# A two-layer block on one core: outputs added in DRAM, the experts' choice spread out, the states of two units summed together

## The chip, the cores and the metric

The kernel runs on one core of a Trainium2 chip. The core has a matrix engine (PE, with its own queue of weight loads, PEld), a vector engine (DVE), an activation engine (ACT), a general engine (POOL), a queue for transfers (SP), and sixteen DMA engines that all queues share. Each engine takes its own instructions in the order of the program and waits on semaphores for the others. The metric is the time of one execution in microseconds (us) on the device; a shorter time is better.

## What is computed

Four sequences of 256 rows by 512 columns go through two layers. Layer 0 is a latent attention with 32 heads and a gated feed-forward network. Layer 1 is a selective state-space scan and a mixture of low-rank experts, both on the normalized input; their results are added to the input. Cut to layer 1, where the change lies:

```python
xn = layernorm(x)
# scan branch: 1024 channels, 16 states each, 256 steps in order
xc = silu(conv4(xn @ in_proj_x)); z = xn @ in_proj_z
dt, Bm, Cm = ...                      # from xc, normalized
h  = exp(dt * A) * h + dt * Bm * xc   # step after step
ys = sum_n(h * Cm)
y  = ((ys + D * xc) * silu(z)) @ out_proj_w.T
# expert branch: 8 experts of rank 16, the best 2 for each row
base   = xn @ base_W.T
probs  = softmax(xn @ router_W.T); top 2, divided by their sum -> w_dense
inc    = (w_dense * (xn @ lora_A)) @ lora_B
out = x + y + base + 2 * inc
```

## The kernel before

Everything is in float32. The scan of one sequence is cut into 8 chunks of 128 channels, and a chunk into 4 *units* of 4 states; so a sequence is 32 units and the whole scan 128 units. A unit works on a tile of 128 partitions by 4 x 256 elements. Below, "unit s20 of sequence 1" is unit 32 + 20 = 52. The program's order is written out by hand: a table tells, for each sequence `b` and each unit `s`, which functions are issued there. Entries of `put(b, s, f, ...)` are issued at the head of the unit, those of `put_mid` between the unit's two DVE instructions, those of `put_late` after them, and those of `put_end` last. `nxt` is the sequence after `b`, whose projections, convolution and step sizes are made while `b` is scanned.

For each unit the loop at the end of the program issues:

- `decays` (L968, ACT): four exponentials, issued three units ahead into one of four buffers;
- `scan_in` (L983, DVE): first a wait for everything that the scan needs, then the product `bx` (L991) of the B rows (`brow`, in PSUM) and the step inputs (`dus`, brought from DRAM by SP);
- `scan` (L996, DVE): the scan itself, `h <- decay, bx` (L1005), then on POOL the product of the states with the C rows, `h <- h, cr` (L1010);
- `states_sum(u - 1)` (L1016, PE): four matmuls in 32-column tiles (L1022) that add the states of the unit before into `ysum` in PSUM; the first unit of a chunk also starts the sum with a full-width matmul `ysum <- xc, dgs` (L1020). After a chunk's last unit `take_sum` (L1025, ACT) copies `ysum` out, and POOL multiplies it with the gate (L1030).

The states `h` lie in four buffers in turn. So the wait at the head of `scan_in(u)` asks, among other things, that the sum of unit u - 4 be done:

```python
for j in (*first, made["da", u], made["hc", u - 4], made["sum", u - 4]):
    tc.add_manual_dep(i.ins, j.ins.name, early, reason="the scan's waits")
```

Around the scan lie, on the same engines: for `nxt`, `norm_stats` (DVE), `px_mm` (L759, PE, input projections), `conv_in` and `conv_taps` (L806, the convolution as matmuls with diagonals that ACT makes), `conv_silu` (L822, ACT, one Silu over the whole sequence), `pp_mm` (L833, PE, at units s17 and s18, from the Silu's result), `pp_square` and `pp_norm` (L847, DVE, at s21); `step_in`, `step_exp`, `step_out`, `step_x`, `send` and `spread` make the step sizes on ACT and POOL and send them through DRAM on the SP queue.

The experts: `router` (L1036) gives scores and low-rank products for two sequences at a time. `route_exp` (s23) and `route` (s25) choose the experts for two sequences, in b = 0 and b = 2, as one run of DVE instructions between two units; `route` also weighs the low-rank products (`mid`, L1089). One output block is a group of 128 rows; there are eight. Its PSUM tile `po` takes, over many units, `dense` (L1109, four matmuls), `expert_out` (L1112: one matmul with the identity that adds `x`, one with `lora_B`) and `out_mm` (L1117, eight matmuls, one for each chunk), and is then copied by `out_x` to SBUF and stored once. Every such float32 matmul is two passes in the profile. The pool of these PSUM tiles (`psmm`) has three buffers, which all the projections share.

Of the kernel before, what the change touches and what calls it, by code (L numbers as in the profile page):

```python
# [8 lines left out]
F32 = mybir.dt.float32  # L9
# [8 lines left out]
P = 128  # L18
# [23 lines left out]
def block_kernel(  # L42
# [675 lines left out]
    def norm_stats(b):  # L718
        mv = w1.tile([P, 2, 2], F32, tag="mv1", name="mv1", bufs=2)
        for i in range(2):  # L720
            st = w1.tile([P, 6], F32, tag="st1", name="st1", bufs=2)
            nc.vector.bn_stats(st, x[:, 2 * b + i, :])
            nc.vector.bn_aggr(mv[:, i, :], st)
        rs = w1.tile([P, 2], F32, tag="rsn", name="rsn", bufs=2)
        inv_root(rs, mv[:, :, 1], eps[:, 0:1])
        live["ln", b] = mv, rs
# [319 lines left out]
    m1 = w1.tile([P, NR], F32, name="m1")  # L1046
    b2 = w1.tile([P, NR], F32, name="b2")
    ex = w1.tile([P, NR, NE], F32, name="ex")
    sel2 = w1.tile([P, NR, NE], F32, name="sel2")
# [5 lines left out]
    def first_of(out, tmp, val, top):  # L1055

        nc.vector.tensor_reduce(top, val, AX.X, ALU.max)
        nc.vector.tensor_tensor(tmp, val, over(top), ALU.is_equal)
        nc.vector.tensor_tensor(tmp, tmp, rev, ALU.mult)
        nc.vector.tensor_reduce(m1, tmp, AX.X, ALU.max)  # L1060
        nc.vector.tensor_tensor(out, tmp, over(m1), ALU.is_equal)

    def route_exp(b):
        lg = live["ml"][:, :, 0:NE]
        nc.vector.tensor_reduce(m1, lg, AX.X, ALU.max)
        nc.vector.tensor_tensor(ex, lg, over(m1), ALU.subtract)
        nc.scalar.activation(ex, ex, AF.Exp)

    def route(b):

        w = psx.tile([P, NG, S], F32, tag="bx", name="w")
        m2 = w[:, 0, 0:NR]
        sel, best, tmp = (
            w[:, k, 0 : NR * NE].rearrange("p (i e) -> p i e", e=NE) for k in (1, 2, 3)
        )
        first_of(sel, sel, ex, m2)

        nc.vector.scalar_tensor_tensor(best, sel, -4.0, ex, ALU.mult, ALU.add)
        first_of(sel2, tmp, best, b2)
        nc.vector.tensor_tensor(sel, sel, sel2, ALU.add)  # L1080
        nc.vector.tensor_tensor(sel, sel, ex, ALU.mult)
        nc.vector.tensor_tensor(m2, m2, b2, ALU.add)
        nc.vector.reciprocal(b2, m2)

        nc.vector.scalar_tensor_tensor(sel, sel, 2.0, over(b2), ALU.mult, ALU.mult)
        for n in range(2):
            mid = act.tile([P, 2, NE, LR], F32, tag="mid", name="mid", bufs=2)
            for i in (2 * n, 2 * n + 1):
                nc.vector.tensor_tensor(  # L1089
                    mid[:, i % 2], live["ml"][:, i, NE:].rearrange("p (e r) -> p e r", r=LR),  # L1090
                    sel[:, i, :].unsqueeze(2).to_broadcast([P, NE, LR]), ALU.mult,
                )
            live["mid", b + n] = mid
# [17 lines left out]

    def expert_out(b, i):  # L1112
        mm(live["po", b, i], lhsT=ident, rhs=x[:, 2 * b + i, :], start=False, stop=False)
        mm(live["po", b, i], lhsT=live["mt"][:, i * P : (i + 1) * P], rhs=late_w["lb"],
           start=False, stop=False)

    def out_mm(b, i, c):  # L1117
        mm(live["po", b, i], lhsT=xcs[b][:, c, i * P : (i + 1) * P], rhs=late_w["ow"][:, c, :],  # L1118
           start=False, stop=(c == DC - 1))

    def out_x(b, i, side=0):
        tb = 2 * b + i
        (nc.vector.tensor_copy if side else nc.scalar.copy)(x[:, tb, :], live.pop(("po", b, i)))
        (nc.scalar if side else nc.sync).dma_start(out_d[tb * P : (tb + 1) * P, :], x[:, tb, :])
# [413 lines left out]
```

## Time and profile before

| | |
|---|---|
| median of 5 runs | 836.7 us (836.08 to 838.71) |
| the profiled execution's own time | 836.34 us |
| its span, first to last instruction | 834.6 us |
| busy: PE / DVE / ACT / POOL | 748.9 / 654.7 / 554.2 / 496.8 us |
| first `bx` to the last scan's end (the scan phase) | 326.15 to 826.2 us |
| DVE busy from 440 to 466 us | 25.48 of 26 us |
| weight transfer issued from POOL (256 KB) | 0.556 us of POOL each |

The span is what lies between the first and the last instruction; the execution's own time has 1.74 us more around it. The profile names a group by its line, its engine and its tiles (out <- in), then how often it ran, its busy time, the mean of one in ns, and the idle time of its engine just before it with what ended that idle time. Busy time is no proof of a bound: PE is counted busy for 90% of the span, and it waits in order like all others. The timeline view gives start, duration and, in brackets, the idle time just before and its releaser.

### The profile page before, as it was taken

What the parts mean: (1) busy time and instruction counts of PE and PEld (TensorE: products, weight loads), DVE (VectorE), ACT (ScalarE), POOL (GpSimd) and SP (SyncE); (2) the same over time, 40 slices, a digit from 0 to 9 for tenths busy, and PEclk for the clock granted to TensorE, in tenths of its full rate; (3) what the DMA queues carried; (4) which work ended last, traced back from release to release, by engine and by line L of the source; (5) the groups of instructions that cost most, each with busy time, mean ns of one, the idle gap of its engine ahead of it and who ended that gap; (6) DMA issues with size and microseconds to landing.
All of it is one profiled execution on the core that took longest, in us unless ns stands there. A gap on an engine that the chain in (4) does not pass through costs nothing.

```text
span 834.6 us, 11274 instructions
## 1 busy us (share of the span) xinstructions
PE 748.9 (90%) x3846; PEld 429.8 (51%) x3846; DVE 654.7 (78%) x604; ACT 554.2 (66%) x1124; POOL 496.8 (60%) x390
## 2 busy tenths in 40 slices
PE   4999999999999999989897899898999978976885
PEld 2665545666555676656553357444457544422331
DVE  4486755288634535798689999989999889999996
ACT  4335574435556277599896898778898787776560
POOL 3233322001343333677968799859899769798775
PEclk9899999999999999979999999889999998898997
DMA  7233332001222322555394745424654443444410
GB/s 227 64 102 114 89 101 63 1 1 38 77 76 78 117 57 64 150 121 147 95 222 126 177 131 135 127 62 116 164 160 122 110 100 97 107 126 128 113 26 26
DMA packets 68645, 86.72 MB, mean 104 GB/s; under 512 B 12222, under 2 KB 52170, under 8 KB 68459
## 3 DMA queue, kind: packets, MB, share of 16 engines
q1 hardware_dynamic: 58794, 65.81, 30.4%
q0 software_dynamic: 9072, 18.35, 7.9%
q10 hardware_dynamic: 720, 1.84, 0.6%
q8 instruction: 30, 0.49, 0.3%
q14 instruction: 29, 0.23, 0.1%
HBM read 66.58 MB, written 10.22 MB: 92 GB/s over the span
## 4 chain that ended last, share of the span: by engine, by line
PE 50%; DVE 22%; POOL 8%; ACT 7%; DMA 6%; issue 5%; SPq 1%; ACTq 0%; POOLq 0%; DVEq 0%
DVE h L1005 10%; PE pg L444 7%; DVE bx L991 6%; PE pu L444 5%; PE px L759 5%; POOL h L1010 4%; PE av L397 4%; PE ysum L1022 3%; PE po L1118 3%; DMA dus<-dud 3%; PE po L469 3%; PE pz L949 3%; PE px L806 3%; PE scT L386 2%; DVE mpl L354 2%
## 5 line engine op out<-in xcount | busy, mean ns | idle before, releaser
L1010 POOL TENSOR_TENSOR h<-h,cr 128x1024 f32<-128x1024 f32 (+1 forms) x130 | 302.0, 2326 | 71.8 <-DVE h L1005 59.3
L1005 DVE TENSOR_TENSOR_SCAN h<-decay,bx 128x1024 f32<-128x1024 f32 (+1 forms) x129 | 288.1, 2235 | 8.5 <-PE po L469 3.6
L979 ACT ACTIVATE decay<-dts,aneg 128x255 f32<-128x255 f32 x504 | 212.4, 500 | 43.1 <-DVE h L1005 29.4
L991 DVE TENSOR_TENSOR bx<-brow,dus 128x1024 f32<-128x1024 f32 x128 | 157.7, 1232 | 18.8 <-PE ysum L1022 7.7
L1022 PE MATMUL ysum<-h,stack 128*32 128x256 f32 x1024 | 87.4, 416 | 34.6 <-POOL h L1010 34.6
L456 POOL TENSOR_TENSOR hlo<-g,hhi 128x512 fp32r<-128x512 f32 x28 | 35.9, 1281 | 114.2 <-ACT hhi L455 114.2
L354 DVE TENSOR_REDUCE mpl<-sc 128x4 f32<-128x1024 f32 x64 | 76.7, 1219 | 22.4 <-PE sc L352 21.0
L427 POOL DMA_DIRECT2D wgu<-in_wgu x56 | 31.1, 556 | 95.3 <-PE pg L444 94.1
L388 ACT ACTIVATE pe<-scT 128x1024 f32<-128x1024 f32 x64 | 64.0, 1023 | 22.9 <-PE sc L352 14.2
L1118 PE MATMUL po<-ow,xc 128*128 128x512 f32 x128 | 69.9, 653 | 2.0 <-POOL xc L1030 1.6
L1022 PEld LDWEIGHTS ysum<-h,stack 128*32 128x32 f32 x1024 | 21.2, 111 | 93.8 <-POOL h L1010 58.3
L949 PE MATMUL pz<-xn1T,w_in 128*128 128x256 f32 x256 | 69.2, 419 | 0.0
L759 PE MATMUL px<-xn1T,w_in 128*128 128x256 f32 x256 | 61.9, 388 | 0.4 <-ACT sz L955 0.3
L949 PEld LDWEIGHTS pz<-xn1T,w_in 128*128 128x128 f32 x256 | 50.4, 206 | 20.5 <-issue 11.8
L759 PEld LDWEIGHTS px<-xn1T,w_in 128*128 128x128 f32 x256 | 48.2, 192 | 13.8 <-issue 3.9
L452 DVE SCALAR_TENSOR_TENSOR g<-g,pg 128x512 f32<-128x512 f32 x28 | 19.2, 687 | 43.0 <-ACT g L451 43.0
L444 PE MATMUL pg<-xhi,wgu 128*128 128x512 f32 x112 | 49.6, 443 | 1.4 <-ACT xhi L244 1.4
L469 PE MATMUL po<-wd,hhi 128*128 128x512 f32 x112 | 49.3, 440 | 0.0
L444 PE MATMUL pu<-xhi,wgu 128*128 128x512 f32 x112 | 47.3, 423 | 0.8 <-DVE g L454 0.8
L455 ACT CAST hhi<-g 128x512 fp32r<-128x512 f32 x28 | 17.3, 619 | 45.8 <-DVE g L454 45.8
L444 PE MATMUL pg<-xlo,wgu 128*128 128x512 f32 x112 | 45.2, 404 | 0.7 <-DVE xlo L251 0.7
L469 PE MATMUL po<-wd,hlo 128*128 128x512 f32 x112 | 44.3, 395 | 0.0
(237 smaller groups left out, 1277.4 us busy)
## 6 DMA issues: line engine op xcount, KB each, us to landing
dts<-dtd SPq DMA_DIRECT2D x124, 128.0 KB, 3.2
dus<-dud SPq DMA_DIRECT2D x124, 128.0 KB, 3.2
wgu<-in_wgu POOLq DMA_DIRECT2D x56, 256.0 KB, 2.8
w_in<-in_inz SPq DMA_DIRECT2D x16, 512.0 KB, 5.5
w_in<-in_inx SPq DMA_DIRECT2D x14, 512.0 KB, 4.5
dtd<-dt SPq DMA_DIRECT2D x15, 256.0 KB, 2.2
dud<-du SPq DMA_DIRECT2D x15, 256.0 KB, 2.3
wd<-in_wd POOLq DMA_DIRECT2D x7, 512.0 KB, 3.6
```

What stands on the lines that cost most here:

```text
L354: nc.vector.tensor_reduce(mpl2[b % 2][:, qb, 2 * hp : 2 * hp + 2, 16 + 2 * gq : 18 + 2 * gq], sc.rearrange("p i (f k) -> p i f k", f=2), A ...
L388: nc.scalar.activation(pes[b, k][:, 2 * t : 2 * t + 2, :], sc, AF.Exp)
L444: mm(ps, lhsT=wgus[i][:, hc, :], rhs=xs[j][:, hc, :], start=(hc == 0 and j == 0), stop=(hc == HC - 1 and j == 1))
L469: mm(po, lhsT=hids[th][j][:, m, i * P : (i + 1) * P], rhs=wd[:, m, :], start=False, stop=(m == MC - 1 and j == 1))
L759: mm(px[:, i, :], lhsT=w[:, i, hc, :], rhs=xns[b][:, hc, :], start=(hc == 0), stop=(hc == HC - 1))
L949: mm(pz[:, i, :], lhsT=w[:, i, hc, :], rhs=xns[b][:, hc, :], start=(hc == 0), stop=(hc == HC - 1))
L979: made["da", u] = nc.scalar.activation(da[:, k, 1:], live["dts", b, c][:, k, 1:], AF.Exp, scale=aneg[:, c, k, g : g + 1])
L991: nc.vector.tensor_tensor(bx, brow[g // 2][:, g % 2, :].unsqueeze(1).to_broadcast([P, NG, S]), live["dus", b, c], ALU.mult)
L1005: nc.vector.tensor_tensor_scan(h[:, n].rearrange("p n t -> p (n t)"), da[:, n].rearrange("p n t -> p (n t)"), bx[:, n].rearrange("p n t -> ...
L1010: made["hc", u] = (nc.vector if k == NG - 1 else nc.gpsimd).tensor_tensor(h[:, n], h[:, n], crows[b][:, g, :].unsqueeze(1).to_broadcast([P ...
L1022: made["sum", u] = mm(ysum[k * NB : (k + 1) * NB, :], lhsT=stack, rhs=hc[:, k, :], start=False, stop=(g == NU - 1))
L1118: mm(live["po", b, i], lhsT=xcs[b][:, c, i * P : (i + 1) * P], rhs=late_w["ow"][:, c, :], start=False, stop=(c == DC - 1))
```

## The change

1. **Sums in pairs.** After every second unit the sums of the last two units are issued together, instead of one after each unit.
2. **Choice one operation at a time.** `route_exp` and `route` become a generator of fifteen DVE instructions, one issued at a time between or after the two DVE instructions of units s22 to s32. It takes the difference to the best score, and the exponential of one number per row. The low-rank products are weighed on POOL (`expert_mid`), in two instructions for four blocks.
3. **Outputs by accumulating transfers.** For sequences 0 to 2 the block `x` is stored early (`store_x`, SP, in b = 0), and the dense and expert part on the one hand, the output projection on the other, each get a PSUM tile of their own, are copied by ACT and added in DRAM by a transfer from POOL (`add_out`). The identity matmul stays only for the last sequence. `dense`, `expert_turn` and `expert_out` of b - 1 move to units s0 to s3 of b; the `out_mm` of sequences 0 to 2 move to other units.
4. **Smaller moves.** The statistics of sequence 2 (`norm_stats`) move from s0 of b = 1 to s3 of b = 0, and three `step_out` and one `step_x` entry move later.

```diff
     def norm_stats(b):
-        mv = w1.tile([P, 2, 2], F32, tag="mv1", name="mv1", bufs=2)
+        mv = w1.tile([P, 2, 2], F32, tag="mv1", name="mv1", bufs=3)
...
+    def norm_root(b):
...
-    def route_exp(b):
...
-    def route(b):
...
+    def route():
+        vec_ = nc.vector
+        lg = live["ml"][:, :, 0:NE]
+        vec_.tensor_reduce(m1, lg, AX.X, ALU.max)
+        yield
+        vec_.tensor_tensor(dl, lg, over(m1), ALU.subtract)
+        yield
+        vec_.scalar_tensor_tensor(sel1, dl, 0.0, rev, ALU.is_equal, ALU.mult)
+        yield
...
+        vec_.tensor_reduce(b2, dl, AX.X, ALU.max)
+        nc.scalar.activation(e2, b2, AF.Exp)
+        nc.scalar.activation(m1, e2, AF.Identity, bias=1.0)
+        yield
...
+        vec_.scalar_tensor_tensor(sel1, sel1, 2.0, over(m1), ALU.mult, ALU.mult)
+        yield
+
+    def expert_mid(b, n):
+        mid = act.tile([P, 2, NE, LR], F32, tag="mid", name="mid", bufs=2)
+        i = slice(2 * n, 2 * n + 2)
+        nc.gpsimd.tensor_tensor(
+            mid, live["ml"][:, i, NE:].rearrange("p i (e r) -> p i e r", r=LR),
+            sel1[:, i, :].unsqueeze(3).to_broadcast([P, 2, NE, LR]), ALU.mult,
         )
...
+    def store_x(tb):
+        stored[tb] = nc.sync.dma_start(rows_of(tb), x[:, tb, :])
+
+    def add_out(tb, po):
+        nc.scalar.copy(x[:, tb, :], po)
+        d = nc.gpsimd.dma_start(rows_of(tb), x[:, tb, :], accum_op=ALU.add)
+        tc.add_manual_dep(d.ins, stored[tb].ins.name, early, reason="sums in place")
+        stored[tb] = d
+
     def expert_out(b, i):
-        mm(live["po", b, i], lhsT=ident, rhs=x[:, 2 * b + i, :], start=False, stop=False)
-        mm(live["po", b, i], lhsT=live["mt"][:, i * P : (i + 1) * P], rhs=late_w["lb"],
-           start=False, stop=False)
+        po, last = live["po", b, i], b == B - 1
+        if last:
+            mm(po, lhsT=ident, rhs=x[:, 2 * b + i, :], start=False, stop=False)
+        mm(po, lhsT=live["mt"][:, i * P : (i + 1) * P], rhs=late_w["lb"], start=False, stop=not last)
+        if not last:
+            add_out(2 * b + i, live.pop(("po", b, i)))
 
     def out_mm(b, i, c):
+        if c == 0 and b < B - 1:
+            live["po", b, i] = psmm.tile([P, D], F32, tag="mm", name="po2")
...
+        if c == DC - 1 and b < B - 1:
+            add_out(2 * b + i, live.pop(("po", b, i)))
...
-            for c in range(DC):
-                put(b, c // 2, out_mm, b - 1, 1, c)
-            put(b, 3, out_x, b - 1, 1)
-            put(b, 4, dense, b - 1, 0, 0)
-            put(b, 5, dense, b - 1, 0, 1)
-            put(b, 5, expert_out, b - 1, 0)
-            for c in range(DC):
-                put(b, 6 + c if c < 2 or nxt == B else 14 + c, out_mm, b - 1, 0, c)
-            put(b, 15 if nxt == B else 23, out_x, b - 1, 0)
+            put(b, 0, gate_silu, b, 0, 1)
+            for k, u in enumerate((0, 1, 1, 2)):
+                put(b, u, dense, b - 1, k // 2, k % 2)
+            put(b, 2, expert_turn, b - 1)
+            for i in range(2):
+                put(b, 3, expert_out, b - 1, i)
+            for (bo_, i), us in {
+                1: {(0, 0): range(22, 30)},
+                2: {(0, 1): (4, 4, 4, 5, 5, 5, 6, 7)},
+                3: {(1, 0): (4, 4, 4, 5, 5, 5, 6, 6), (1, 1): (6, 7, 7, 7, 8, 8, 8, 9),
+                    (2, 0): (9, 9, 10, 10, 10, 11, 11, 11), (2, 1): (12, 12, 12, 13, 13, 13, 14, 15)},
+            }[b].items():
+                for c, u in enumerate(us):
+                    put(b, u, out_mm, bo_, i, c)
...
+            for tb in range(NTB - 2):
+                put(b, 8 + tb // 2, store_x, tb)
...
-            put(b, 0 if b else 2, norm_stats, nxt)
+            if nxt == 2:
+                put_mid(0, 3, norm_stats, nxt)
+            else:
+                put(b, 0 if b else 2, norm_stats, nxt)
+            put(b, 0 if b else 2, norm_root, nxt)
...
-                put(b, 25, route, b)
-            put(b, 26, expert_turn, b)
-            put(b, 25, dense, b, 1, 0)
-            put(b, 26, dense, b, 1, 1)
-            put(b, 28, expert_out, b, 1)
+                choice = route()
+                for w, u in ((0, 22), (0, 23), (0, 24), (1, 25), (0, 25), (0, 26), (1, 27), (0, 27),
+                             (0, 28), (1, 29), (0, 29), (1, 30), (0, 30), (0, 31), (0, 32)):
+                    (put_mid if w else put_late)(b, u, next, choice)
+                for i in range(2):
+                    put_late(b, 32 + i, expert_mid, b, i)
...
-        if 1 <= u <= total:
+        if u and u % 2 == 0:
+            states_sum(u - 2)
             states_sum(u - 1)
```

## The prediction

> **What bounds the kernel now.** I read the page's groups first, then the waits by engine, then the timeline of DVE and of PE in the scan phase. The groups name the loop's four costs (line, engine, out <- in, count, busy, mean ns, idle before):
>
> ```profile
> L1010 POOL TENSOR_TENSOR h<-h,cr 128x1024 f32<-128x1024 f32 (+1 forms) x130 | 302.0, 2326 | 71.8 <-DVE h L1005 59.3
> L1005 DVE TENSOR_TENSOR_SCAN h<-decay,bx 128x1024 f32<-128x1024 f32 (+1 forms) x129 | 288.1, 2235 | 8.5 <-PE po L469 3.6
> L991 DVE TENSOR_TENSOR bx<-brow,dus 128x1024 f32<-128x1024 f32 x128 | 157.7, 1232 | 18.8 <-PE ysum L1022 7.7
> L1022 PE MATMUL ysum<-h,stack 128*32 128x256 f32 x1024 | 87.4, 416 | 34.6 <-POOL h L1010 34.6
> ```
>
> Undisturbed units follow each other at 3.59 us (`bx` at 523.72, 527.31, 530.89): 1.23 + 2.29 + 0.07. POOL idles mostly until DVE's scan. So DVE bounds the scan phase, and only what lengthens a unit counts. From the first `bx` (326.15) to the last (822.50) lie 127 units, 496.4 us; 127 x 3.588 is 455.7. The excess of 40.7, summed from the starts of `bx`: units 0 to 5 of sequence 0, 8.0; units 6 to 21 of sequence 0, 10.7; the choice at s22 and s24, 4.8 in sequence 0 and 6.3 in sequence 2; s20 and s21, 3.84 in sequence 1 and 2.52 in sequence 2; the statistics at s31, 1.71 and 2.50; the rest 0.3. The waits (total us, times, longest) say who ends them:
>
> ```profile
> DVE bx L991 <- PE ysum L1022: 7.7, 6, 2.3
> DVE bx L991 <- DMA dus<-dud: 5.2, 3, 3.5
> DVE h L1005 <- PE po L469: 3.6, 1, 3.6
> DVE w L1057 <- ACT ex L1067: 1.6, 1, 1.6
> ```
>
> PE is the engine that DVE waits for, though not for want of time alone: in-order PE waits 14.5 us in 8 places for ACT to copy `ysum` out.
>
> **Choice.** The run that goes, in DVE's timeline of sequence 0:
>
> ```profile
> 434.86 0.19 DVE L1057 TENSOR_REDUCE w<-ex 128x4 f32<-128x32 f32 x1
> ...
> 438.27 0.20 DVE L1085 SCALAR_TENSOR_TENSOR w<-w,b 128x32 f32<-128x32 f32 x1
> 438.51 0.88 DVE L1089 TENSOR_TENSOR mid<-ml,w 128x128 f32<-128x128 f32 x4
> 439.42 1.23 DVE L991 TENSOR_TENSOR bx<-brow,dus 128x1024 f32<-128x1024 f32 x1
> ```
>
> Both runs together cost 4.8 + 6.3 = 11.1, the second with 1.57 of waiting for ACT's exponential. Fifteen instructions of 0.20 come back per choice. One lone 0.13 instruction at s1 (`sh`) lengthens its unit to 3.66, by 0.07; the two of s22 (0.16 and 0.19) lengthen theirs by 0.19. So a 0.20 one costs 0.10 to its full 0.20; I take 0.14, nearer the rows: 30 x 0.14 = 4.2 (3.0 to 6.0). **-6.9** (-8.1 to -5.1). The exponential of `b2` on ACT is asked for by the reciprocal three units later; ACT stands three units ahead by its decays, which hides it. `mid` becomes four POOL instructions of the gate's form (L1030, 128x256, 0.727): 2.9 us of POOL, hidden, since POOL has 3.59 - 2.37 = 1.2 free in each unit before side work; without that cover, 2.9.
>
> **Statistics of sequence 2.** 0.66 + 0.18, twice, gave 1.71. At s3 of sequence 0 they delay `scan(3)`, but `scan(4)` waits 3.6 for PE's last `po` (L469), so they cost nothing there; without that wait, 1.7. **-1.7**. The first sums of the loop, issued together, let PE end that `po` some 0.5 sooner: **-0.5** (0 to -1).
>
> **Pairs, the gain.** PE in sequence 1:
>
> ```profile
> 508.78 1.89 PE L806 MATMUL px<-pad,tap 128*128 128x256 f32 x8
> 510.51 1.89 PE L759 MATMUL px<-xn1T,w_in 128*128 128x256 f32 x8
> 512.33 0.64 PE L1022 MATMUL ysum<-h,stack 128*32 128x256 f32 x8
> 512.90 1.99 PE L759 MATMUL px<-xn1T,w_in 128*128 128x256 f32 x8
> ```
>
> Group after group starts 1.73 later; with a sum between, 1.82 + 0.57 = 2.39, so a sum costs 0.66. Of its 0.64 some 0.41 is the idle time to the next full-width load, so a second sum in the same group should add about 0.23: 0.9 for a pair instead of 1.32, 27 us of PE over 64 pairs. It pays only where PE holds DVE up:
>
> ```profile
> 530.11 1.12 PE L1118 MATMUL po<-ow,xc 128*128 128x512 f32 x2
> 534.31 1.22 PE L1020 MATMUL ysum<-xc,dgs 128*128 128x256 f32 x2 [3.07 <-ACT xc L1027]
> ...
> 536.47 3.68 PE L833 MATMUL pp<-xc,xpw 128*64 128x256 f32 x8
> 541.26 1.94 PE L833 MATMUL pp<-xc,xpw 128*64 128x256 f32 x8
> 543.13 0.64 PE L1022 MATMUL ysum<-h,stack 128*32 128x256 f32 x8
> 543.97 1.23 DVE L991 TENSOR_TENSOR bx<-brow,dus 128x1024 f32<-128x1024 f32 x1 [2.35 <-PE ysum L1022]
> 546.39 0.48 DVE L847 SCALAR_TENSOR_TENSOR nrm<-pp,lnw,rs 64x256 f32<-64x256 f32 x1 [1.19 <-ACT rs L715]
> ```
>
> PE stands idle for the copy (3.07), although the Silu that `pp` needs ended at 532.09; then `bx` of s21 waits for the sum of s17, and `nrm` for what follows `pp`. Afterwards L1020 of s16 stands behind both `pp`, and the two `out_mm` of s18 and s19 are gone. `pp` from 532.1: 3.68 + 1.94 = 537.7; L1020 and the sum of s16, about 0.9: 538.6. `bx` of s20 stood at 538.07, so it waits 0.6, s21 and `nrm` no more; `nrm` itself keeps 0.4. 3.84 becomes 1.0: **-2.8** (-3.4 to 0). In sequence 2, where the wait was 2.52: **-1.3** (-2.1 to 0).
>
> **Pairs, the cost.** For even u the sum of u - 4 now comes behind PE's work of one unit more; this speaks against the change. In sequence 0, `bx` of s12 started at 377.59 without a wait, while that of s13 waited for the sum of s9 until 382.88. That sum stands behind the convolution matmuls of s10, which start when ACT has made the diagonals (376.66). Now the sum of s8 stands there too, so s12 starts at about 383.2 and s13 at 386.8, 3.9 later. PE and ACT pace this stage as before; a wait for `dus` (s20, 414.89) swallows some, but the sum of s16 now lies behind both `pp` (413.65, 5.35, cold after 3.9 idle) and L1020, so s20 starts near 420.3 and s21 near 424, not 419.77. **+4.0** (0 if the saved PE time arrives first, +6). In sequences 1 and 2, s11 and s12 hold 1.8 + 3.6 + 1.8 of matmuls and a pair of 0.9: 8.1 in two units of 7.18. **+1.4** each (0 to 4).
>
> **Outputs.** PE loses six identity matmuls of two passes (0.59 each): 7 us, off the path. ACT gets six more copies of 0.576 and the moved `mt` copy. SP's seven stores stay seven, six of them at s8 to s10, ahead of spreads that have units to spare. POOL gets twelve transfers, of which the only row is a plain load:
>
> ```profile
> L427 POOL DMA_DIRECT2D wgu<-in_wgu x56: 527/558/746, 8.5 to 276.1; - x56
> ```
>
> I take 0.56 each, 6.7 in all; no row accumulates, so the cost may lie between 0.56 and the 2.8 that such a load takes to land. At s3 two of them stand behind ACT's copies, and behind them waits POOL's product of s3. The decays of s6 ended in sequence 1 at 1.0 into s4; two copies more make 2.2, so the product ends about 5.7 after its scan, not 2.55. A product had 8.3 to spare before the scan four units on: no cost there.
>
> The Trainium skill ("DMA: Bandwidth & Descriptors", Specifications) gives a first byte after about 1 us for POOL's software path and 0.6 for SP's, which speaks against moving stores to POOL. This case's trace has 0.556 of POOL for the issue. By the page's figure the twelve would hold POOL for 12 us, by the row for 6.7; the sum would be the same by both, as the slack covers either.
>
> ACT: the decays of s7 had 3.34, 1.50 and 1.74 to spare in sequences 1 to 3. Two copies (0.9) and the lost cover of the long choice eat that in two sequences: **+1.5** (0 to 4). In sequence 3, s4 to s13 hold three `out_mm` each: 0.955 x 3 (two take 1.91 at 469.90) + 0.45 + 0.14 = 3.5 of 3.59, where PE was busy 12.4 of 21 us (733 to 754). It just fits: **+0.7** (0 to 4).
>
> **Sum.** -6.9 - 1.7 - 0.5 - 2.8 - 1.3 + 4.0 + 2.8 + 1.5 + 0.7 = -4.2. The profiled execution took 836.34 (its span 834.6 and 1.74 around it), the median of the runs is 836.7; on the median: **832.5**.
>
> **Rivals.**
> - *The freed PE time carries through.* For it: DVE's largest releaser is PE; 27 us and up to 14.5 us of waiting go. Then ACT's diagonals come sooner, and the +4.0, +2.8, +1.5 and +0.7 fall away: -13.2, 823.5. Against it: in sequence 0, ACT was busy without a gap from 353.5 to 372, and PE cannot hurry that.
> - *The even scans decide (slower).* Place: `scan_in` at even units from s8 to s20. It decides once PE ends a pair over 7.18 after the even unit's start. Seq 0 then loses 6, sequences 1 and 2 lose 4 each, and the gain at s20 is nil: -6.9 - 1.7 - 0.5 + 14 + 1.5 + 0.7 = +7.1, 843.8. For it: the sum of s10 had 3.6 to spare at s14, about one unit's work. Against it: PE saves 0.4 in every pair.
> - *POOL is held by the transfers.* If an accumulating issue costs 2 to 2.8, four between s6 and s15 of sequence 3 and the pairs at s3 push products past their 8.3, about +4 on the forecast: 836.7. Against it: the 0.56 row.
>
> **How the numbers follow.** Forecast 0.50, freed PE 0.22, even scans 0.16, POOL 0.12. The forecast's own range, its open terms together, is 827 to 838. The whole range leaves out half of each outer case, about 0.2: 823 to 842. Within 0.2% (835.0 to 838.4) the kernel can't be told from the one before. Faster: 0.40 + 0.22 = 0.62. Same: 0.08 of the forecast and 0.07 of POOL = 0.15. Slower: 0.02 + 0.16 + 0.05 = 0.23.
>
> **What would show it.** Right: no run of small DVE instructions and lone 0.20 ones in units of about 3.7; no statistics at s31 of sequence 0; PE's wait for `ysum`'s copy gone before `pp`; `bx` of s12 and s20 in sequence 0 waiting for sums, at even units. Wrong: waits of `bx` for POOL's product, issues of `out <- x` far over 0.6, or DVE units of 3.59 through all of s8 to s21.

## The result and the profile after

The changed kernel takes 838.5 us (median of 50 runs) beside 836.4 for the kernel before; the ratio is 1.0034, with a 95% interval of 1.0023 to 1.0044. The ratio goes by all runs, and 0.0034 of 836.4 is 2.8 us (the medians alone are 2.1 apart): the change is slower by 2.8 us, where the prediction said faster by 4.2. The profiled execution's span is 837.1 us (834.6 before).

The costliest groups of the loop in the changed kernel's page (busy us, mean ns, idle before):

```profile
L1014 POOL TENSOR_TENSOR h<-h,cr 128x1024 f32<-128x1024 f32 (+1 forms) x130 | 312.1, 2426 | 59.3 <-DVE h L1009 47.3
L1009 DVE TENSOR_TENSOR_SCAN h<-decay,bx 128x1024 f32<-128x1024 f32 (+1 forms) x129 | 288.1, 2235 | 6.2 <-PE po L469 1.6
L995 DVE TENSOR_TENSOR bx<-brow,dus 128x1024 f32<-128x1024 f32 x128 | 157.6, 1231 | 33.1 <-PE ysum L1026 10.8
L1026 PE MATMUL ysum<-h,stack 128*32 128x256 f32 x1024 | 80.3, 413 | 35.6 <-POOL h L1014 35.6
```

PE's sums cost less (80.3 us, 87.4 before), and DVE's scan is untouched. But DVE's idle time before `bx` has gone from 18.8 to 33.1 us. The view of waits (us, times, longest) names several releasers for it:

```profile
DVE bx L995 <- PE ysum L1026: 10.8, 4, 6.6
DVE bx L995 <- ACT dg L780: 6.2, 2, 4.6
DVE bx L995 <- ACT decay L983: 5.1, 4, 3.0
DVE bx L995 <- DMA rl<-in_rl: 2.7, 1, 2.7
```

Of these only the first is right. The diagonals (`dg`), the decays and the load had long been done; in the timeline, from s7 of sequence 0 on, `bx` starts 0.20 to 0.26 us after PE's sum of the unit four back wherever it waits for 0.3 us or more, and every such place is an even unit. The starts of `bx` give the excess over 3.588 us per unit:

| units | before | after |
|---|---|---|
| 0 to 5 of sequence 0 | 8.0 | 7.7 |
| 6 to 21 of sequence 0 | 10.7 | 18.5 |
| s22 of sequence 0 to s0 of sequence 1 (choice, statistics) | 6.5 | 1.9 |
| s1 to s19 of sequence 1 | 0.1 | 3.5 |
| s20, s21 of sequence 1 | 3.9 | 0.3 |
| s22 to s31 of sequence 1 | 2.5 | 3.9 |
| s0 to s19 of sequence 2 | 0.1 | 2.6 |
| s20, s21 of sequence 2 | 2.5 | 0.3 |
| s22 of sequence 2 to s0 of sequence 3 (choice) | 6.4 | 1.0 |
| the rest of sequence 3 | 0.1 | 2.9 |
| all 127 | 40.7 | 42.5 |

What the change was to take out of the choice, the statistics and s20 is gone: 15.8 us. It came back in the convolution stage of sequence 0 (+7.8) and in small waits over sequences 1 to 3.

### The profile page after: what moved, and what is told of

Same layout as the page of the kernel before. It is cut to its first block, busy times and chain, and to the rows that moved or that the text cites. A ratio compares the mean times of both kernels' runs of the same rounds, so it can differ in the third digit from the quotient of the medians.

```text
span 837.1 us, 11252 instructions
## 1 busy us (share of the span) xinstructions
PE 737.7 (88%) x3834; PEld 441.1 (53%) x3834; DVE 649.7 (78%) x590; ACT 557.3 (67%) x1132; POOL 509.6 (61%) x406
## 4 chain that ended last, share of the span: by engine, by line
PE 48%; DVE 18%; ACT 12%; POOL 12%; issue 6%; DMA 3%; SPq 1%; POOLq 0%; ACTq 0%; DVEq 0%
DVE h L1009 7%; POOL h L1014 7%; PE pg L444 6%; PE pu L444 5%; DVE bx L995 5%; PE av L397 4%; ACT decay L983 4%; PE po L469 3%; PE pz L953 3%; PE ysum L1026 3%; PE px L763 3%; PE px L810 2%; PE scT L386 2%; PE po L1119 2%; DVE mpl L354 2%
## 5 line engine op out<-in xcount | busy, mean ns | idle before, releaser
L1014 POOL TENSOR_TENSOR h<-h,cr 128x1024 f32<-128x1024 f32 (+1 forms) x130 | 312.1, 2426 | 59.3 <-DVE h L1009 47.3
L995 DVE TENSOR_TENSOR bx<-brow,dus 128x1024 f32<-128x1024 f32 x128 | 157.6, 1231 | 33.1 <-PE ysum L1026 10.8
L1026 PE MATMUL ysum<-h,stack 128*32 128x256 f32 x1024 | 80.3, 413 | 35.6 <-POOL h L1014 35.6
L1026 PEld LDWEIGHTS ysum<-h,stack 128*32 128x32 f32 x1024 | 25.0, 112 | 82.1 <-POOL h L1014 52.9
L1148 PE MATMUL po<-ow,xc 128*128 128x512 f32 x128 | 64.7, 643 | 0.4 <-DVE xc L1446 0.4
L763 PEld LDWEIGHTS px<-xn1T,w_in 128*128 128x128 f32 x256 | 50.1, 198 | 16.8 <-ACT xn1T L755 6.2
L444 PE MATMUL pu<-xlo,wgu 128*128 128x512 f32 x112 | 44.4, 396 | 0.0
```

The costliest lines, as they stand in the source:

```text
L444: mm(ps, lhsT=wgus[i][:, hc, :], rhs=xs[j][:, hc, :], start=(hc == 0 and j == 0), stop=(hc == HC - 1 and j == 1))
L763: mm(px[:, i, :], lhsT=w[:, i, hc, :], rhs=xns[b][:, hc, :], start=(hc == 0), stop=(hc == HC - 1))
L995: nc.vector.tensor_tensor(bx, brow[g // 2][:, g % 2, :].unsqueeze(1).to_broadcast([P, NG, S]), live["dus", b, c], ALU.mult)
L1014: made["hc", u] = (nc.vector if k == NG - 1 else nc.gpsimd).tensor_tensor(h[:, n], h[:, n], crows[b][:, g, :].unsqueeze(1).to_broadcast([P ...
L1026: made["sum", u] = mm(ysum[k * NB : (k + 1) * NB, :], lhsT=stack, rhs=hc[:, k, :], start=False, stop=(g == NU - 1))
```

## The experiments

Each ratio is to the kernel before, on the same chip, with its 95% interval; 0.001 is 0.84 us. "Excess" is the measure of the table above, from one profile of each run.

**Pairs and transfers, each with and without.** `a_single` puts the sums of single units back, `a_noadd` leaves the accumulating transfers out, `a_single_noadd` does both.

```
-        if u and u % 2 == 0:
-            states_sum(u - 2)
+        if 1 <= u <= total:
             states_sum(u - 1)
```
```
         nc.scalar.copy(x[:, tb, :], po)
-        d = nc.gpsimd.dma_start(rows_of(tb), x[:, tb, :], accum_op=ALU.add)
-        tc.add_manual_dep(d.ins, stored[tb].ins.name, early, reason="sums in place")
-        stored[tb] = d
```

> The changed kernel with one sum after every unit again, all else as changed. Theory 'pairs' (an even unit's sum comes one unit of PE work later, and DVE waits for it): the waits at even units of sequence 0 (18.4 us there after the change, 10.7 before) go back by 7.7, those at s8 and s24 of sequence 1 (2.9 and 2.2), s14 and s20 of sequence 2 (1.7 and 0.9) and s4 to s20 of sequence 3 (2.9) go, some 3 us come back at s20 and s21 of sequence 1: about 828, ratio to before 0.990. Rival 'POOL' (its longer queue makes the products, and so the sums, late): the waits stay whoever issues the sums, 836 to 839, ratio 1.000 to 1.003. Rival 'freed PE' (pairs save PE time and that is worth more than it costs): 841 or more, ratio over 1.005.

> The changed kernel without POOL's accumulating transfers (the outputs lack the sums that they add; the copies to x stay). Theory 'pairs': POOL's issues lie in its slack, no change, 838 within 1, ratio 1.002 to 1.004. Rival 'POOL': the lag of its products (6 to 9 us after the scans at s3 to s12 of sequences 1 and 3, 5 to 6 elsewhere) falls and with it the waits in sequences 1 and 3, -4 to -8, ratio 0.993 to 0.998.

> The changed kernel with single sums and without POOL's accumulating transfers (the outputs lack the sums that they add). If the transfers are the whole cost of the outputs: 825.7, ratio 0.987. If they are half of it, and PE's and ACT's moved work the other half: 829.5, ratio 0.992. If only the moved work costs: 833, ratio 0.996 as with the transfers.

| ratio | pairs | single sums |
|---|---|---|
| with the transfers | 1.0034 (1.0023 to 1.0044) | 0.9959 (0.9941 to 0.9978) |
| without them | 0.998 (0.9958 to 1.0002) | 0.9903 (0.989 to 0.9917) |

Pairs cost 6.3 us with the transfers and 6.4 without; the transfers cost 4.5 with pairs and 4.7 without. Within the intervals, some 2 us for each difference, the two costs simply add. Theory "pairs" had the sign, but with 828 too large a gain; that POOL's issues lie in its slack was wrong.

**Where the pairs cost.** `b_pairs` is the kernel before with pairs alone (the first diff above, reversed). `a_pairs_not0` is the changed kernel with pairs only where `u // PER > 0`:

```
+    summed = 0
...
-        if u and u % 2 == 0:
-            states_sum(u - 2)
-            states_sum(u - 1)
+        if 1 <= u <= total and not (u % 2 and u // PER > 0):
+            while summed < u:
+                states_sum(summed)
+                summed += 1
```

> The kernel before with the sums in pairs alone. Theory 'pairs': +7.7 in sequence 0, less up to 3.6 at s20 and s21 of sequence 1, and some waits at even units elsewhere: 840 to 844, ratio 1.005 to 1.009. The prediction's own terms (-0.5 -2.8 -1.3 +4.0 +2.8) give +2.2, ratio 1.003. Rival 'freed PE': -4.6, ratio 0.994. Rival 'POOL': without the new transfers and copies pairs cost nothing, ratio 1.000 or below.

> The changed kernel with single sums in sequence 0 and pairs in sequences 1 to 3. Theory 'pairs cost in sequence 0 alone': its 7.8 us go, the rest stays as it is in the changed kernel (s8 and s24 of sequence 1, sequence 3, and the gain at s20 and s21): ratio 0.994, below the 0.996 of single sums throughout. Rival 'pairs cost everywhere': half of 6.3 us goes, ratio 0.9995, above single sums throughout.

Measured: 1.0033 (1.0013 to 1.0053) and 0.9942 (0.9923 to 0.9962). Single sums in sequence 0 alone give 7.7 us back, which is what the table shows there, and pairs in the other three sequences gain 1.4 against `a_single`, less than the intervals can tell from nothing. In `b_pairs` the profile has +7.8 in units 6 to 21 of sequence 0, and -3.6, -2.3 at s20 and s21 of sequences 1 and 2; in sequence 2 most of that comes back close by, 2.0 at s19 and 1.8 at s23. Alone, pairs cost 2.8 us, not the 6.3 that they cost in the changed kernel.

How 7.8 us come about is to be read from the first of these waits. PE and DVE in the changed kernel, s7 and s8 of sequence 0 (start, us, engine, line):

```profile
361.84 2.07 PE L876 MATMUL pdt<-nrm,dtw 32*128 32x256 f32 x4 [1.77 <-ACT dt L882]
...
363.84 1.22 PE L1024 MATMUL ysum<-xc,dgs 128*128 128x256 f32 x2
...
364.99 1.94 PE L1026 MATMUL ysum<-h,stack 128*32 128x256 f32 x16
...
366.33 1.23 DVE L995 TENSOR_TENSOR bx<-brow,dus 128x1024 f32<-128x1024 f32 x1 [2.74 <-DMA rl<-in_rl]
```

and the same place in the kernel before:

```profile
360.32 1.08 PE L1022 MATMUL ysum<-h,stack 128*32 128x256 f32 x8
...
361.34 2.07 PE L872 MATMUL pdt<-nrm,dtw 32*128 32x256 f32 x4
...
363.09 1.23 DVE L991 TENSOR_TENSOR bx<-brow,dus 128x1024 f32<-128x1024 f32 x1
...
363.34 1.08 PE L1022 MATMUL ysum<-h,stack 128*32 128x256 f32 x8
```

Before, the sum of s4 ran ahead of `pdt`, and `bx` of s8 (363.09) didn't wait. Now the pair, the sums of s4 and s5, stands behind `pdt`, and `pdt` waits 1.77 us for ACT; the products for the first half of the pair were ready before that. `bx` of s8 waits 2.74 (the load that the view names was not what it waited for: the first half of the pair, the sum of s4, ended 0.26 before it). From there on the stage goes round in waits. PE's waits for ACT and ACT's for PE in the stage, after (356 to 425 us):

```profile
PE pp L837 <- ACT xc L826: 4.9, 1, 4.9
...
PE px L810 <- ACT xc L788: 2.0, 1, 2.0
PE pdt L876 <- ACT dt L882: 1.8, 1, 1.8
...
ACT ml L1047 <- PE pr L1045: 3.2, 1, 3.2
ACT xc L1031 <- PE ysum L1026: 2.9, 2, 2.1
```

and before (356 to 420 us):

```profile
PE pp L833 <- ACT xc L822: 3.9, 1, 3.9
...
PE px L806 <- ACT xc L784: 0.7, 1, 0.7
...
ACT ml L1043 <- PE pr L1041: 2.3, 1, 2.3
ACT xc L1027 <- PE ysum L1022: 1.4, 2, 1.1
```

The view by windows (PE, PEld, DVE, ACT and POOL busy, then the share of its full clock that PE was granted), after and before:

```profile
356.00:425.00 69.00, 57.27 (x309) 40.90 (x310) 49.70 (x30) 59.71 (x132) 52.13 (x33) 0.85 0.57 154
```
```profile
356.00:420.00 64.00, 57.42 (x310) 38.68 (x310) 52.72 (x31) 58.99 (x132) 53.13 (x34) 0.89 0.49 124
```

PE is busy for as long as before to within 0.2 us, ACT to within 0.8; each waits longer for the other. But PE's equal busy time is not equal work. The sums take 8.4 us instead of 9.8, and what they save is lost on the matmuls that follow a wait: `pp` takes 6.0 instead of 5.4, those with the diagonals 8.5 instead of 8.0. In these windows the clock was granted at half rate for 20.5 us after and 13.7 before, and each such stretch that begins in the stage began when PE had been idle for 2.0 to 3.0 of the 3.4 us ahead of it. So longer waits went with a slower PE; by an estimate (half of the 6.8 us more) that is some 3 us of PE's work. The clock's share of the 7.8 us is not separated from that of the waits by any run. Over whole runs, the granted clock was 0.937 on average in the changed kernel and in `b_pairs`, 0.951 in the kernel before and 0.946 in `a_pairs_not0`; in the kernel before too, runs with a lower clock were longer (831.2 us at 0.964, 838.5 at 0.950).

**The choice.** `a_oldchoice` is the changed kernel with the old `route_exp` at s23 and `route` at s25; in it the exponential came behind the step's own at s23. `a_oldchoice2` has it ahead of them, as before. `b_choice_stats` is the kernel before with the new choice and the moved statistics; parts of its edit:

```
+            if b % 2:
+                put(b, 2, expert_turn, b - 1)
...
+                    put(b, 3, expert_out, b - 1, 1)
...
-                put(b, 25, route, b)
+                choice = route()
...
+                    put_late(b, 32 + i, expert_mid, b, i)
```

> The changed kernel with the old choice (a run of DVE instructions at s25, products for mid on DVE), all else as changed. If the choice gains what its own units show (11.1 of excess before, 2.1 after): +9, 847.5, ratio to before 1.013. If it gains the 6.9 predicted: 845.4, ratio 1.011. If the run of the choice only gave slack that is lost elsewhere (PE catches up behind it): +4 or less, ratio under 1.008.

> As a_oldchoice, but the exponential asked for ahead of the step's own, as in the kernel before. If the choice in the changed kernel gains what the old one cost less what the new one costs in its own units (11.1 less 2.1): +9, ratio 1.014. If 2.3 of that was the exponential's place: +6.7, ratio 1.011. If the old run of DVE instructions also gave PE and POOL time to catch up, which the lone instructions don't: +4 or less, ratio below 1.008.

> The kernel before with the new choice (its three neighbours that give it room too: two step_out, one step_x, and the even sequences' turn and second lora product behind the choice) and the moved statistics; sums one at a time and outputs as before. Theory 'outputs' (what the choice and the statistics gain is given back by the outputs' part of the change): -9.0 for the choice, -1.7 for the statistics, 825.7, ratio to before 0.987. Rival 'choice smaller' (the units of the choice hide a cost that appears elsewhere): 0.996, the ratio of the changed kernel with single sums.

Measured: 1.0132 (1.0097 to 1.0167), 1.0103 (1.0083 to 1.0124), and 0.9934 (0.9915 to 0.9952). Within the changed kernel the choice gains 5.8 us; choice and statistics in the old surroundings 5.5. Its own units show more: 11.1 before, 2.1 after. Most lone instructions cost nothing at all, since a unit with one of 0.17 us stays at 3.58; the 2.1 lie in a few that ran far longer. One of them, DVE and POOL in the changed kernel at s27 of sequence 0:

```profile
454.22 1.26 POOL L931 TENSOR_TENSOR du<-dt,xc 128x512 f32<-128x512 f32 x1
454.57 0.96 DVE L1078 TENSOR_TENSOR sel<-dl,b 128x32 f32<-128x32 f32 x1
455.44 2.34 POOL L1014 TENSOR_TENSOR h<-h,cr 128x1024 f32<-128x1024 f32 x1
455.46 1.22 DVE L995 TENSOR_TENSOR bx<-brow,dus 128x1024 f32<-128x1024 f32 x1
```

It ends when POOL's instruction does (455.48, plus 0.05). In `b_choice_stats`, where POOL lags 7.2 us behind the scans at s24 to s26 of sequence 2, the same instruction took 1.91 and the next 0.85, each to 0.05 after the end of a POOL product, and the units of the choice there have an excess of 4.4. What the choice gains is thus not one number: against `outputs_alone2` (below), which has the outputs' part and the old choice, `a_single` with the new choice and the moved statistics gains 11.9 us (1.0101 to 0.9959).

**The outputs alone.** `outputs_alone` and `outputs_alone2` are the kernel before with the outputs' part of the change alone; the second has the exponential in its old place. The second against the first:

```
             put(b, 22, c_rows, nxt, 0)
+            if b % 2 == 0:
+                put(b, 23, route_exp, b)
             put(b, 23, step_exp, nxt, 0, slice(0, 2))
...
-                put(b, 23, route_exp, b)
                 put(b, 25, route, b)
```

> The kernel before with the outputs' part alone (dense products at s0 to s2 of the next sequence, sums stored apart, accumulating transfers on POOL); choice, statistics and single sums as before. Theory 'outputs': +7, 843, ratio 1.008, with POOL's products lagging 6 to 10 us behind their scans from s3 to s17 of sequences 1 to 3. Rival 'no cost there' (the prediction's own step, 0 and +1.5 and +0.7 for ACT and PE): at most +2.2, ratio 1.003 or below.

> As outputs_alone, but the old choice's exponential is asked for ahead of the step's exponentials at s23, as in the kernel before (in outputs_alone it stood behind them, which cost 3.5 and 2.0 us at s24 of sequences 0 and 2). The outputs' part alone: 1.0216 less 5.5 us is a ratio of 1.015. Rival (the prediction's terms for it, +2.2): 1.003.

Measured: 1.0216 (1.0198 to 1.0235) and 1.0101 (1.0076 to 1.0125). The first is spoilt by the exponential. The second says 8.4 us, not the 2.2 of the prediction, and not 12.5 either. Beside the new choice the same part costs only 2.1 (`b_choice_stats` 0.9934 to `a_single` 0.9959). POOL's products end 6.8 to 10.8 us after their scans from s3 to s14 of sequences 1 to 3 (before: 2.5 to 5.2).

**What a transfer on POOL costs.** `b_pooladd` makes seven plain stores of the kernel before accumulating ones on POOL's queue, `b_poolstore` plain ones there. The edit of the second (the first also gives `accum_op=ALU.add`):

```
-        (nc.scalar if side else nc.sync).dma_start(out_d[tb * P : (tb + 1) * P, :], x[:, tb, :])
+        (nc.scalar if side else nc.gpsimd).dma_start(out_d[tb * P : (tb + 1) * P, :], x[:, tb, :])
```

> The kernel before with its seven stores of SP's queue made accumulating transfers on POOL's (the output then holds sums with what lay there before); nothing else is moved. Theory 'a transfer slows POOL': the two to seven products after each issue take 2.6 to 3.0 us instead of 2.35, some 20 of 130 above 2.45, and the time rises little, ratio 1.000 to 1.004. Rival (products are slow in the changed kernel because of what was moved beside them): all products stay at 2.35, ratio 0.998 to 1.001.

> The kernel before with its seven stores of SP's queue on POOL's, plain, without accumulation. Theory 'any transfer on POOL's queue slows POOL': products of 2.6 to 2.7 us for 20 to 30 us after each issue, some 30 of 130 above 2.45, and a ratio near the 1.008 of b_pooladd, half of it at the end, where the last store lands later. Rival 'the accumulation does it': products stay at 2.35 and the ratio is 1.000 to 1.003.

Measured: 1.0079 (1.0051 to 1.0107) and 1.0061 (1.0039 to 1.0083). About half lies at the end: from the last `bx` to the end of the span 15.7 and 15.0 us instead of 12.1, as the last store lands later from POOL's queue. The other half (3.3 and 2.8 us) is in the loop, where POOL stood 12.9 and 16.5 us behind ACT's copies. POOL around its first store, accumulating:

```profile
481.47 0.93 POOL L1127 DMA_DIRECT2D out<-x  x1 [2.21 <-PE ysum L1022]
482.12 5.01 POOL L1010 TENSOR_TENSOR h<-h,cr 128x1024 f32<-128x1024 f32 x2
...
488.00 2.66 POOL L1010 TENSOR_TENSOR h<-h,cr 128x1024 f32<-128x1024 f32 x1
490.32 1.57 POOL L918 TENSOR_TENSOR e<-e,lw 128x512 f32<-128x512 f32 x1
```

and plain:

```profile
480.36 0.61 POOL L1124 DMA_DIRECT2D out<-x  x1 [2.19 <-ACT x L1123]
...
486.88 2.36 POOL L1010 TENSOR_TENSOR h<-h,cr 128x1024 f32<-128x1024 f32 x1
489.20 1.26 POOL L918 TENSOR_TENSOR e<-e,lw 128x512 f32<-128x512 f32 x1
```

The product takes 2.66 by its record in the first and 2.36 in the second, so it is the accumulation, not the queue, that lengthens it. But the next instruction starts 2.32 after it in both. "Slow products", as the expectations have it, is wrong: POOL's pace is unchanged, and only the ends come late.

**How the transfers cost 4.6 us.** `a_single_late` issues each transfer three units after ACT's copy; `a_single_plain` makes the twelve plain.

```
-        d = nc.gpsimd.dma_start(rows_of(tb), x[:, tb, :], accum_op=ALU.add)
...
+        owed.append([3, tb])
...
+            d = nc.gpsimd.dma_start(rows_of(tb), x[:, tb, :], accum_op=ALU.add)
```
```
-        d = nc.gpsimd.dma_start(rows_of(tb), x[:, tb, :], accum_op=ALU.add)
+        d = nc.gpsimd.dma_start(rows_of(tb), x[:, tb, :])
```

> As a_single (0.9959), but each accumulating transfer is issued three units after ACT's copy of its sum, so that POOL doesn't stand behind the copy. Theory 'wait' (POOL in its order behind the copy makes the lag): the lag at s3 falls from 8 to 3 us and the cost of the transfers (0.9959 against 0.9903 without them) goes, 0.991. Theory 'slow products': they stay at 2.6 to 3.0 us for 20 to 30 us, and the ratio stays within 0.994 to 0.996.

> As a_single, but the twelve transfers on POOL's queue are plain stores (the later store of a block overwrites the earlier, so the outputs lack what would be added). As b_poolstore showed, products then stay at 2.35 us and an issue takes 0.58. Theory 'slow products': 0.991 to 0.992. Theory 'wait': 0.994 to 0.996.

Measured: 0.9936 (0.9912 to 0.996) and 0.9944 (0.9926 to 0.9963), between the 0.9959 of `a_single` and the 0.9903 without transfers. Without the wait POOL's lag at s3 falls from 8.3 to 2.5 us as expected, but only some 1.9 us come back. Plain stores, which keep the wait and end the products on time, give 1.3 back, which lies in the range of theory "wait" (0.994 to 0.996) and not in that of "slow products". The late issue brings a loss of its own. POOL and DVE in `a_single_late`, s1 of sequence 2:

```profile
588.94 0.88 POOL L1142 DMA_DIRECT2D out<-x  x1
589.55 1.58 POOL L931 TENSOR_TENSOR du<-dt,xc 128x512 f32<-128x512 f32 x1
...
590.00 3.47 DVE L735 SCALAR_TENSOR_TENSOR sh<-mv,rsn 128x2 f32<-128x2 f32 x1
...
590.78 2.65 POOL L1014 TENSOR_TENSOR h<-h,cr 128x1024 f32<-128x1024 f32 x1
...
593.40 1.22 DVE L995 TENSOR_TENSOR bx<-brow,dus 128x1024 f32<-128x1024 f32 x1
```

The small `sh` (0.13 us in the kernel before) ends only after two of POOL's instructions, and its unit loses 3.3 us, where `a_single` loses 0.3. The excess of the whole loop is 36.6 us; less this place it is 33.3, beside 33.9 without transfers and 36.9 in `a_single`. So by the profiles the wait behind ACT's copies can account for the whole cost. It is worked out from one profile of each, and no run has the late issue without that loss: argued, not shown. PE's view agrees in direction: its sums wait 30.4 us in all for POOL's products in `a_single`, 20.2 without transfers, 25.1 with the late issue (35.6 and 23.4 in the changed kernel with and without transfers).

**Better versions.** `b_best` is `b_choice_stats` with pairs from s16 to s21 of sequences 1 and 2. `a_ident` is `a_single` with identity matmuls and one store on SP in place of the transfers; `a_ident_hyb` adds pairs from s8 to s21 of sequences 1 and 2, `a_ident_hyb2` of sequence 2 alone.

```
         if c == 0 and b < B - 1:
             live["po", b, i] = psmm.tile([P, D], F32, tag="mm", name="po2")
+            mm(live["po", b, i], lhsT=ident, rhs=x[:, 2 * b + i, :], start=True, stop=False)
...
         if c == DC - 1 and b < B - 1:
-            add_out(2 * b + i, live.pop(("po", b, i)))
+            out_x(b, i)
```

> The kernel before with the new choice, the moved statistics, and pairs only from s16 to s21 of sequences 1 and 2; elsewhere one sum after every unit, outputs as before. Theory 'pairs cost where PE paces the conv stage of sequence 0 and pay where pp stands behind the copy': the 3.6 and 2.3 at s20 and s21 come on top of 10.7: 820, ratio 0.980. Rival (the pairs' gain there needs the outputs' products gone from s18 and s19): 824 to 826, ratio 0.985 to 0.987.

> The changed kernel with single sums, and with identity matmuls in place of the accumulating transfers: expert_out adds x as before and is copied to x by ACT, the first out_mm of a block adds that x again, and one store on SP's queue sends the sum; places of the dense products and of out_mm as in the changed kernel. If the transfers cost what the two pairs of runs show (4.6 us) and 12 identity matmuls of 0.6 lie off the path: ratio 0.990 to 0.992. Rival (PE is near its bound there): the 7 us of PE count in part, 0.995 or more.

> As a_ident, with the sums in pairs from s8 to s21 of sequences 1 and 2 alone. If pairs gain where pp stands behind the copy and PE had saved time before it (the kernel before with pairs: 3.6 and 2.3 us at s20 and s21): 0.984 to 0.987. Rival (pairs move the wait from s20 and s21 to s19, as in b_best, or to s13): the ratio of a_ident.

> As a_ident, with the sums in pairs from s8 to s21 of sequence 2 alone. In a_ident_hyb's profile the pairs lost 2.0 at s19 and 3.4 at s23 of sequence 1 and saved 2.7 in sequence 2. Theory 'pairs pay where no out_mm lies near pp': 0.986 to 0.987. Rival (a_ident_hyb gained by its pairs in sequence 1 too): 0.988 or more.

Measured: 0.9925 (0.9905 to 0.9945), 0.9895 (0.9871 to 0.9919), 0.9871 (0.9845 to 0.9896) and 0.9863 (0.9837 to 0.9888). `b_best` gains nothing over `b_choice_stats` that its interval shows: the waits go from s20 and s21 to s19 (2.5 and 4.6 us in sequences 1 and 2). With the output products moved away and the transfers gone, `a_ident` beats the kernel before by 1.0% and the changed one by 1.4%, and `a_ident_hyb2`, 825.3 us beside 836.0, by 1.4%. What is left to wait for in its profile:

```profile
DVE bx L995 <- PE ysum L1026: 7.8, 8, 2.4
DVE bx L995 <- DMA dus<-dud: 5.4, 4, 3.5
DVE bx L995 <- ACT decay L983: 1.7, 1, 1.7
```

## Why the prediction was wrong

The runs form a ladder from the kernel before to the changed one: `b_choice_stats` 0.9934, `a_single_noadd` 0.9903, `a_single` 0.9959, the change 1.0034. Each rung beside the prediction's terms for it (us):

| part | predicted | measured |
|---|---|---|
| choice and statistics (-6.9 -1.7) | -8.6 | -5.5 |
| outputs without the transfers (ACT +1.5, sequence 3 +0.7) | +2.2 | -2.6 |
| transfers | 0 | +4.7 |
| pairs (-0.5 -2.8 -1.3 +4.0 +2.8) | +2.2 | +6.3 |
| sum (of unrounded terms) | -4.2 | +2.8 |

Each measured rung is uncertain by some 2 us, and the ladder is one order of several. Alone on the kernel before, pairs cost 2.8 (`b_pairs`), close to the predicted 2.2, and the outputs with their transfers 8.4 (`outputs_alone2`) where the ladder has 2.1; choice and statistics gain 5.5 there and 11.9 on top of the outputs. The prediction added the parts as if each had one price, and they don't. That the pairs' 2.2 was met when alone is luck: its parts were +7.8 for +4.0 in sequence 0, -5.9 for -4.1 at s20 and s21, +3.8 at s19 and s23 of sequence 2, which it didn't name, nothing for the +2.8 at s12 to s14, and 2.3 gained at s24 of sequence 2 and s31 of sequence 1, which it didn't name either.

Two steps failed. Had either cost what was predicted, the rungs would add up to a gain (2.8 less 3.8 for the first, 2.8 less 4.7 for the second).

- **"Pairs, the cost: +4.0 (0 to +6)"** measured +7.7 to +7.8, outside its bounds. It followed the late sum to s12 and s20 only. The stage already loses 2.8 at s8 and 1.6 at s10, and s16 waits 4.5 where 0.7 and 2.3 were lost at s16 and s17 before. "PE and ACT pace this stage as before" was the wrong sentence: with hardly more busy time the stage took longer, since PE's late sum delays ACT's copy, ACT's late results delay PE, and PE ran at half rate for longer.
- **"A product had 8.3 to spare before the scan four units on: no cost there."** The lag came as worked out (5.7 foretold at s3 of sequence 1; 7.5 in the profile), and 0.6 of POOL per issue was right. But the spare time was counted to the scan alone. Between product and scan stands PE, in order: its sum waits for the product, and all that PE has behind it waits too. The lag was also not a matter of one unit. From s5 to s14 POOL's side work leaves it no time to catch up. That the transfers cost 4.7 is shown by leaving them out; that it is by this path rests on PE's waits and on the subtraction above.

A chain of both at s3 to s8 of sequence 1 in the changed kernel:

```profile
488.06 1.85 POOL L1133 DMA_DIRECT2D out<-x  x2 [3.64 <-ACT x L1132]
...
492.34 0.64 PE L1026 MATMUL ysum<-h,stack 128*32 128x256 f32 x8 [3.02 <-POOL h L1014]
...
497.27 3.63 PE L763 MATMUL px<-xn1T,w_in 128*128 128x256 f32 x8 [4.29 <-ACT xn1T L755]
...
501.26 1.07 PE L1026 MATMUL ysum<-h,stack 128*32 128x256 f32 x16
...
502.16 1.23 DVE L995 TENSOR_TENSOR bx<-brow,dus 128x1024 f32<-128x1024 f32 x1 [2.99 <-ACT decay L983]
```

POOL waits 3.64 for ACT's copies, PE 3.02 for POOL's product, then 4.29 for ACT's copy of `xn1T`, behind ACT's decays; the pair with the sum of s4 comes after that, and `bx` of s8 loses 3.0. Single sums lose nothing at this place (`a_single`), nor do pairs without the moved outputs (`b_pairs`); without the transfers it is 3.7 (`a_noadd`). So it takes the pairs and the moved outputs together to make this wait; the transfers are not needed for it.

The other steps:

- *Choice, -6.9.* Right in sign. Of 0.14 per lone instruction most was nothing; of the 2.1 that remain, 1.4 are two instructions held up by POOL, which the prediction didn't know of. Shown by undoing it: 5.8.
- *Statistics, -1.7; first sums, -0.5.* Right: s31 of sequence 0 lost 1.71 before and nothing after, and s3 and s4 together 4.70 and 4.38. The first sums gave 0.3.
- *s20 and s21, -2.8 and -1.3.* The places lost 3.6 and 2.3 less. With single sums (`a_single`) they had already fallen from 3.9 to 1.9 and from 2.5 to 0.9, but s17 and s19 lost 2.1 and 1.1 in their stead, where nothing was lost before; so from s17 to s21 it is the pairs that gain, 3.7 and 0.8.
- *s12 to s14 of sequences 1 and 2, +1.4 each.* 0 and 1.65, and the latter is not the pairs': it is 1.80 with single sums (`a_single`) and nothing without the transfers (`a_noadd`).
- *ACT's lateness at s7, +1.5.* The place was right in sequence 1 (3.0); the wait was for the late pair, as the decays still had 1.2 to spare. Sequence 2 lost nothing there, sequence 3 0.7.
- *Sequence 3, +0.7.* 2.9 in the change, 0.5 without the transfers: PE did fit, POOL didn't.

The "27 us of PE over 64 pairs" were about twice too much. In `b_pairs`, where PE runs group after group, a pair takes 1.00 us to the start of the next full-width group:

```profile
507.29 1.07 PE L1022 MATMUL ysum<-h,stack 128*32 128x256 f32 x16
508.29 2.00 PE L806 MATMUL px<-pad,dg 128*128 128x256 f32 x8
```

One sum took 0.57 (512.33 to 512.90 in the prediction's lines). So the second adds 0.43, not 0.23, and a pair saves 0.23, not 0.42: some 15 us over 64 pairs, by estimate. "PE saves 0.4 in every pair", held against the rival of the even scans, was as much too large.

Of the rivals, "the even scans decide" had the mechanism and for sequence 0 nearly the price (7.8 for 6), but in sequences 1 and 2 even units lost 3.0 (s8) and 2.5 (s14 and s20) up to s20, not 4 each, and the gain at s20, which it held to be nil, came. "POOL is held by the transfers" had the size (+4) at an issue time of 2 to 2.8 us that didn't come; POOL went on after 0.56 to 0.63, where nothing else held it. So the 12 us that the prediction worked out from a first-byte time as POOL's hold were not seen either. Both rivals together, set against the gain of the choice, give the result; the prediction held them for alternatives.

## What to carry to other kernels

The spare time of an instruction is to be counted to every consumer in its chain, in the order of each in-order engine on the way, and over all units for which the debt lasts; counted to the last consumer alone it hides the cost. Batching two results to save an engine's time delays the first of them by one batch, and where two engines wait for each other in turns, that delay comes back in each turn while the saved time is spent waiting. The price of a part alone is not its price beside the others: 8.4 us alone became 2.1 here, and 2.8 became 6.3. Costs found for alternatives can occur together: two rivals with different places should be added before the sign is forecast.

## What the runs showed of the hardware

- After an accumulating transfer is issued from POOL, POOL's instructions end late but start on time. In the changed kernel 29 products over 2.45 us that were followed at once by another instruction are recorded with 2.78 us on average, 68 others of the same size with 2.37; the next instruction starts after 2.34 and 2.32. One transfer makes it 2.5 to 2.7 (`b_pooladd` and the change). Two issued together made it 2.9 to 3.0 in sequences 1 and 2 of the change, but 2.7 in sequence 3. It lasts for 5 to 30 us after an issue, though the transfers landed after 3.7 to 6.5. The late end is real for others: where PE had been waiting, it mostly started its sum 0.05 us after the recorded end, late or not. With plain stores on the same queue (`b_poolstore`) all products stayed at 2.33 to 2.39.
- An issue of an accumulating transfer is recorded with 0.80 to 1.19 us, but POOL's next instruction usually starts 0.56 to 0.63 us after it, as after a plain one (0.55 to 0.66). The Trainium skill ("Perfetto Trace Analysis", GPSIMD Engine Instruction) advises to time POOL by the spacing of starts rather than by spans; for POOL's pace the rows above agree, for its consumers the end counts.
- A DVE instruction with two operands in SBUF that meets a running POOL instruction ends 0.05 us after that one does (0.96 and 1.91 us instead of 0.17; 3.47 for `sh`, which met two in a row), while reductions and reciprocals with one operand ran beside POOL's product in 0.17, and the old choice, with operands in PSUM, in 0.20. The Trainium skill ("SBUF — State Buffer", SBUF: two separate sides) describes an exclusive lock on a pair of ports that DVE and POOL share, for DVE instructions with two inputs in SBUF; these rows agree with it.
